# Layer 1, first pass: where the variance products and their transposes stand in the loop over strips

## The chip, the cores and the metric

The kernel runs on one core of a Trainium2 chip. The metric is the time of one execution on the device, in microseconds (us); lower is better. The engines are named as in the profile: PE is TensorE (PEld its weight loads), DVE is VectorE, ACT is ScalarE, POOL is GpSimd, and SP issues the DMAs.

## The reference

Two layers run one after the other on an image of 4 x 64 x 256 x 256 float32. Each adds to its input a function of the group-normed input. Layer 0 is a gated convolution with a small FFT; the change does not touch it. Layer 1 reads the image once along rows and once along columns as a sequence of 65,536 tokens of 64 channels, and does to each:

```python
fx = _layer_norm(x, ln1_g[i], ln1_b[i])            # over the 64 channels of a token
h = _s5_scan(fx, ...)                              # a linear recurrence forward and backward
x = jax.nn.gelu(h) + fx
fx2 = _layer_norm(x, ln2_g[i], ln2_b[i])
return fx2 @ ff_enc[i].T @ ff_dec[i].T + fx2
```

The two results are mixed by a 64 x 128 matrix and added to the input of the layer. What matters here is the first layer norm: the variance of each token over its 64 channels, one over its root, and the product with it.

## The kernel before, in words

For each of the four images, layer 1 runs `pass_a` (the layer norm, and a summary of each piece of 16 tokens for the recurrence), `scan` (the recurrence over the pieces) and `pass_b` (states, filter, second layer norm, output). The change is in `pass_a` alone.

`pass_a` goes over 16 strips of 16 rows. A strip lies in SBUF as 128 partitions (two halves of 64 channels) by 2048 elements, and is treated in four blocks of 512. Its steps:

- `centre(g, i)`: one matmul takes the mean off block i (`pc` in PSUM); ACT writes the centred values `xc` and their squares `sq`.
- `sums(g)`: four matmuls add the squares of the four blocks over the channels, all into one PSUM tile `pv`; ACT copies it to `sums`.
- `rstd_of(g)`: four PE transposes of `sums`, into another `pv` (the pool has one buffer of it); DVE adds the epsilon (`ve`); POOL raises to the power -0.5 (`rs`).
- `widen(g)`: DVE repeats these factors over 64 channels (`rw`, one buffer).
- `affine(g, i)`: four PE transposes bring the factors of block i to the layout of the data (`pr`, two buffers); DVE multiplies (`z`); ACT applies gain and bias twice, for columns (`fv`) and for rows (`fh`).
- `mirrored(s, g)`: SP stores `fv` and `fh`; DVE and POOL each make a sum and a difference of mirrored halves (`sd`, two operations on each engine).
- `summary_columns` and `summary_rows`, in two halves each: matmuls over `sd` into `pt` and `ps`, and with the second half an ACT copy `m` and DVE additions and subtractions `sf`, `sb`.

The steps run as a pipeline over strips. In iteration n, strip n is centred, strip n-1 gets its factors, strip n-2 its affine step, and strip n-3 its summaries; 16 + 3 iterations run for an image. Within an iteration, a loop over i = 0 to 3 interleaves one block of each (lines 1144 to 1156). [...] PE's instructions in this pass are pinned to the order of the program, and the other engines' queues show the same order, up to some small moves (the widening stands ahead of the `sd` of the same iteration, and the DVE work of the row summaries behind them).

The squares have five buffers, so a strip's four and one of the next fit.

Of the kernel before, what the change touches and what calls it, by code (L numbers as in the profile page):

```python
# [108 lines left out]
def tile_kernel(ctx: ExitStack, tc: tile.TileContext, x, cst, w0, winp, wdwp, w1, out):  # L109
# [74 lines left out]
    with ExitStack() as l0:  # L184
# [83 lines left out]
        with ExitStack() as l1w:  # L268
# [35 lines left out]
            def tmp(n=2, dt=F32):  # L304
                n_tmp[0] += 1
                return new(sp, [P, n], f"tmp{n_tmp[0]}", None, dt)
# [49 lines left out]
            def mul(a, b):  # L356
                o = tmp()
                TT(o, a, b, ALU.mult)
                return o
# [176 lines left out]
            u, t, r, i = mul(ur, ur), mul(ui, ui), tmp(), tmp()  # L536
# [9 lines left out]
            n = 1  # L546
# [456 lines left out]
    def load_strip(b, s):  # L1003
        t = new(ring, [P, 8, S], "strip")
        for h, r, row in rows_of(s):
            nc.sync.dma_start(out=t[h, r], in_=x1d[b][:, row : row + 7 : 2, :])
        return t
# [13 lines left out]
    def pass_a(b, x0):  # L1021
        with ExitStack() as es:
# [66 lines left out]
            def mirrored(s, g):  # L1089

                for d, n, e in ((1, 4, nc.vector), (0, 8, nc.gpsimd)):
                    f = g.pop("fv" if d else "fh")
                    nc.sync.dma_start(out=fxd[b][s, d], in_=f.rearrange("p a b -> p (a b)"))
                    for k, op in enumerate((ALU.add, ALU.subtract)):
                        t = g["sd", d, k] = new(wk, [P, n, 1024 // n], f"sd{d}", 3)
                        e.tensor_tensor(t, f[:, :n], f[:, : n - 1 : -1], op)  # L1096
# [43 lines left out]
            def at(s, step, *args):  # L1140
                if 0 <= s < NS1:
                    step(got[s], *args)

            for n in range(NS1 + 3):
                if n + 1 < NS1:
                    got[n + 1] = {"x": load_strip(b, n + 1)}
                for i in range(4):
                    at(n, centre, i)
                    if i == 1:
                        at(n - 1, rstd_of)  # L1150
                    at(n - 2, affine, i)
                    at(n - 3, (summary_columns, summary_rows)[i // 2], n - 3, i % 2)
                at(n, sums)
                if 0 <= n - 2 < NS1:
                    mirrored(n - 2, got[n - 2])
                at(n - 1, widen)
# [309 lines left out]
    for b in range(nb):  # L1466
        pass_a(b, first)
        first = pass_b(b)
# [77 lines left out]
```

## Time and profile before

| what | us |
|---|---|
| median of three runs | 9406.5 |
| lowest and highest of them | 9404.52 and 9409.52 |
| the profiled execution, its own time | 9404.9 |
| its span, from first to last instruction | 9403.1 |
| PE busy in the span | 8799.6 (94%) |
| DVE busy | 7346.4 (78%) |
| POOL busy | 3651.7 (39%) |
| ACT busy | 2785.1 (30%) |

The first matmul of `pass_a` starts at 4587.4, 5784.9, 6989.8 and 8193.7 us for the four images. All sums of an engine are over the whole span; `pass_a` has its own proportions, so its parts are read from stretches of the timeline. In the lines of the timeline the first number is the start in us from the beginning of the span, the second the time from the first start to the last end of the instructions merged in the line, and in square brackets stands the idle time of the engine just before, with what ended it. In the lines of waits, the numbers are the total in us, how often, and the longest. In lines by stretch, there are the length, then busy us and instructions of PE, PEld, DVE, ACT and POOL, the granted clock of PE as a share of its full one, the busy share of the DMA engines and GB/s.

### The profile page before, as it was taken

To read this page: it belongs to the slowest core of one execution; us is meant where nothing else is said; L and a number is where in the kernel's file an instruction comes from. 1 tells how busy PE (TensorE), PEld (TensorE's weight loads), DVE (VectorE), ACT (ScalarE), POOL (GpSimd) and SP (SyncE) were. 2 spreads that over 40 slices of the span, in tenths; PEclk is the share of its full clock that TensorE was granted. 3 is DMA by queue.
4 is the path that set the end of the run, shared out by engine and by line. 5 is a ranking of instruction groups with operands and counts; after the bars stand their busy time and mean duration, and the time that the engine had idled before them with its cause. 6 is when DMAs were issued, how large, how long until landed. Compare 5 with 4: busy or idle time off the path is not lost. (4 is left out here: it accounts for less than half of the span.)

```text
span 9403.1 us, 182768 instructions
## 1 busy us (share of the span) xinstructions
PE 8799.6 (94%) x78454; PEld 5836.8 (62%) x78454; DVE 7346.4 (78%) x8833; ACT 2785.1 (30%) x4570; POOL 3651.7 (39%) x2177
## 2 busy tenths in 40 slices
PE   3999999999999999999899999999999999999999
PEld 2666666666666666666556666556666566665666
DVE  7999989998999988888676776776767777677676
ACT  2222222222222222222452223522236222262222
POOL 4222222222222222222373444744446544375443
PEclk9999999999999999999999999999999999999999
DMA  7444444444434433333442234523346133362322
GB/s 170 97 95 99 99 94 97 97 96 96 99 95 99 97 85 84 83 81 77 121 159 67 78 90 115 183 55 86 79 104 202 50 85 86 86 195 72 90 77 72
DMA packets 655576, 938.40 MB, mean 100 GB/s; under 512 B 43184, under 2 KB 584880, under 8 KB 619184
## 3 DMA queue, kind: packets, MB, share of 16 engines
q1 hardware_dynamic: 654768, 926.71, 38.1%
q8 instruction: 619, 10.14, 0.5%
q14 instruction: 189, 1.55, 0.1%
HBM read 583.86 MB, written 275.05 MB: 91 GB/s over the span
## 5 line engine op out<-in xcount | busy, mean ns | idle before, releaser
L197 PE MATMUL m<-v,sw 64*128 64x256 f32 (+1 forms) x8192 | 1643.1, 414 | 209.6 <-DVE v L625 209.6
L197 PEld LDWEIGHTS m<-v,sw 64*128 64x128 f32 (+1 forms) x8192 | 1160.9, 200 | 769.7 <-DVE v L625 330.5
L1361 POOL TENSOR_TENSOR xr<-xr,fx 128x512 f32<-128x512 f32 x512 | 650.2, 1270 | 1861.7 <-ACT xr L1360 1371.1
L1258 PE MATMUL pst<-fx,wb 64*128 64x256 f32 (+1 forms) x4992 | 1015.9, 438 | 37.3 <-DVE stm L1264 18.3
L156 POOL TENSOR_SCALAR pn<-pr,nm,rs 128x512 f32<-128x512 f32 x256 | 387.5, 1521 | 1411.4 <-PE two L197 1406.2
L625 DVE SCALAR_TENSOR_TENSOR acc<-xat,taps,acc 128x1024 f32<-128x1024 f32 x640 | 831.0, 1298 | 4.6
L625 DVE SCALAR_TENSOR_TENSOR acc<-xen,taps,acc 128x1024 f32<-128x1024 f32 x384 | 750.1, 1953 | 4.5
L1258 PEld LDWEIGHTS pst<-fx,wb 64*128 64x128 f32 (+1 forms) x4992 | 508.1, 187 | 370.8 <-issue 244.2
L797 ACT ACTIVATE ge<-two 128x1024 f32<-128x1024 f32 x256 | 262.8, 1026 | 1593.8 <-PE two L197 1593.7
L1391 POOL TENSOR_TENSOR rs<-ve,mhalf 128x32 f32<-128x32 f32 x128 | 695.2, 5432 | 99.8 <-DVE ve L1264 99.8
L1264 DVE SCALAR_TENSOR_TENSOR stm<-stm,step,pst 128x512 f32<-128x512 f32 x640 | 478.4, 748 | 232.7 <-PE pst L1258 219.2
L197 PEld LDWEIGHTS m<-ct,hw 128*64 128x64 f32 x16384 | 510.6, 138 | 116.9 <-issue 116.9
L1362 ACT ACTIVATE sq<-xr 128x512 f32<-128x512 f32 x512 | 322.6, 630 | 874.5 <-POOL xr L1361 874.5
L1258 PE MATMUL px<-wb,xr 128*128 128x128 f32 x4096 | 574.8, 284 | 0.0
L1264 DVE SCALAR_TENSOR_TENSOR sto<-sto,step,pst 128x512 f32<-128x512 f32 x512 | 382.7, 747 | 242.7 <-PE pst L1258 228.8
L1258 PEld LDWEIGHTS px<-wb,xr 128*128 128x128 f32 x4096 | 524.8, 194 | 54.2 <-issue 41.8
L1264 DVE TENSOR_TENSOR y<-px,rs 128x512 f32<-128x512 f32 x512 | 353.7, 691 | 232.5 <-PE px L1258 222.7
L1258 PE MATMUL ph<-sto,wb 128*64 128x128 f32 (+1 forms) x5120 | 528.0, 299 | 0.0
L197 PE MATMUL m<-ct,hw 128*64 128x64 f32 x16384 | 527.8, 223 | 0.0
L1258 PE MATMUL ph<-stm,wb 128*64 128x128 f32 (+1 forms) x5120 | 525.0, 299 | 0.0
L1258 PEld LDWEIGHTS ph<-stm,wb 128*64 128x64 f32 (+1 forms) x5120 | 409.0, 147 | 144.6 <-issue 128.0
L1096 POOL TENSOR_TENSOR sd<-fh 128x1024 f32<-128x1024 f32 x128 | 380.3, 2991 | 298.4 <-PE pv L1034 225.4
(318 smaller groups left out, 16525.4 us busy)
## 6 DMA issues: line engine op xcount, KB each, us to landing
strip<-x1d SPq DMA_DIRECT2D x512, 256.0 KB, 7.3
fx<-fxd SPq DMA_DIRECT2D x128, 1024.0 KB, 7.0
at<-in_x_dram SPq DMA_DIRECT2D x248, 320.0 KB, 4.9
xen<-xat SPq DMA_DIRECT2D x256, 258.0 KB, 3.7
sx<-in_x_dram SPq DMA_DIRECT2D x256, 256.0 KB, 5.2
pr<-in_x_dram SPq DMA_DIRECT2D x256, 256.0 KB, 4.2
er<-in_x_dram SPq DMA_DIRECT2D x256, 256.0 KB, 4.7
x1d<-x SPq DMA_DIRECT2D x256, 256.0 KB, 3.6
```

Of the source, the lines that this page charges most:

```text
L156: nc.gpsimd.tensor_scalar(o, i, nm, rs, ALU.add, ALU.mult)
L197: tc.keep_in_program_order(nc.tensor.matmul(*args, **kw))
L625: return lambda *args, **kw: tc.keep_in_program_order(getattr(nc.vector, name)(*args, **kw))
L797: nc.scalar.activation(t["ge"], pg.rearrange("p e x -> p (e x)"), AF.Gelu)
L1096: e.tensor_tensor(t, f[:, :n], f[:, : n - 1 : -1], op)
L1258: tc.keep_in_program_order(nc.tensor.matmul(*args, **kw))
L1264: return lambda *args, **kw: tc.keep_in_program_order(getattr(nc.vector, name)(*args, **kw))
L1361: nc.gpsimd.tensor_tensor(xr, xr, fx, ALU.add)
L1362: nc.scalar.activation(sq, xr, AF.Square)
L1391: nc.gpsimd.tensor_tensor(r, ve.rearrange("p n c -> p (n c)"), mhalf, ALU.pow)
```

## The change

In the loop over blocks, `sums` leaves the end of the iteration: for strip n-1 it now runs in iteration n, in block 0 behind that block's `affine` of strip n-2. `rstd_of`, which stood in block 1 ahead of `affine`, now stands in block 1 behind it. The steps themselves are as they were.

```diff
                 for i in range(4):
                     at(n, centre, i)
-                    if i == 1:
-                        at(n - 1, rstd_of)
                     at(n - 2, affine, i)
+                    if i < 2:
+                        at(n - 1, (sums, rstd_of)[i])
                     at(n - 3, (summary_columns, summary_rows)[i // 2], n - 3, i % 2)
-                at(n, sums)
                 if 0 <= n - 2 < NS1:
                     mirrored(n - 2, got[n - 2])
                 at(n - 1, widen)
```

In the order of each engine's instructions, a steady iteration changes so. PE before: centre 0, affine 0, columns, centre 1, transposes of `sums`, affine 1, columns, centre 2, affine 2, rows, centre 3, affine 3, rows, products of the squares. PE after: centre 0, affine 0, products of the squares, columns, centre 1, affine 1, transposes of `sums`, columns, and the rest as before. ACT's copy of `sums` moves from ahead of block 0's `xc` to behind block 0's `fh`. On DVE `ve` moves from ahead of block 1's `z` to behind it. POOL's order does not change in steady iterations.

## The prediction

> **What bounds the kernel now.** I read the page first. TensorE is busy 94% of the span (8799.6 of 9403.1 us), but that is an average over stages, and the change touches one: pass_a, which runs four times, as the matmuls of `pc` (centre) show: from 4587.4, 5784.9, 6989.8 and 8193.7 us, some 280 us each. Then the groups by line: `pv<-sq`, the products of sums, wait 33.4 us in all for ACT's last square, and that is the wait the change takes apart. Whether it matters I asked of the waits and the timeline of one stretch where the passes run steadily, 4660 to 4820 (ten strips).
>
> ```profile
> L1034 PE MATMUL pv<-sq,ct 128*32 128x512 f32 x512 | 141.1, 605 | 34.2 <-ACT sq L1045 33.4
> ```
>
> ```profile
> ACT fv L1080 <- DVE ve L1061: 35.8, 10, 3.6
> DVE sf L1112 <- ACT m L1110: 34.4, 10, 3.4
> DVE sd L1096 <- ACT fv L1080: 14.9, 10, 1.5
> ...
> ACT fv L1080 <- DVE z L1076: 8.4, 10, 0.9
> ...
> PE pv L1034 <- ACT sq L1045: 5.6, 10, 0.6
> ```
>
> PE waits 0.56 us a strip. ACT and DVE wait for each other far longer, 3.6 + 0.9 and 3.4 + 1.5 us: the mark of a loop through both. The timeline of one strip shows it (start, duration):
>
> ```profile
> 4743.70 4.53 DVE L1096 TENSOR_TENSOR sd<-fv 128x1024 f32<-128x1024 f32 x2 [1.49 <-ACT fv L1080]
> ...
> 4744.53 0.59 ACT L1054 COPY sums<-pv 128x512 f32<-128x512 f32 x1
> ...
> 4747.98 0.60 PE L1038 MATMUL pv<-ct,sums 128*128 128x128 f32 x4
> ...
> 4748.95 1.02 DVE L1076 TENSOR_TENSOR z<-xc,pr 128x512 f32<-128x512 f32 x1
> ...
> 4750.00 0.81 ACT L1080 ACTIVATE fv<-z,prm 128x512 f32<-128x512 f32 x1 [3.58 <-DVE ve L1061]
> ...
> 4751.43 0.67 ACT L1044 ACTIVATE xc<-pc,norms 128x512 f32<-128x512 f32 x1
> ...
> 4753.98 0.35 ACT L1110 COPY m<-pt 128x256 f32<-128x256 f32 x1
> ...
> 4754.36 0.60 DVE L1112 TENSOR_TENSOR sf<-pt,m 128x256 f32<-128x256 f32 x1 [3.43 <-ACT m L1110]
> ...
> 4756.32 0.81 ACT L1080 ACTIVATE fv<-z,prm 128x512 f32<-128x512 f32 x1 [0.83 <-DVE z L1076]
> ...
> 4758.89 0.81 ACT L1080 ACTIVATE fv<-z,prm 128x512 f32<-128x512 f32 x1
> ...
> 4759.73 4.52 DVE L1096 TENSOR_TENSOR sd<-fv 128x1024 f32<-128x1024 f32 x2 [1.49 <-ACT fv L1080]
> ```
>
> From one `sd` to the next: sd and the four row results on DVE until z of block 0, 5.25; z to fv, 1.05; fv, fh, xc, sq, fv, fh on ACT until m, 3.98; m to sf, 0.38; sf, sb and z of block 2 until its fv, 1.96; fv, fh, xc, sq until fv of block 3, 2.57; fv to sd, 0.84. The sum is 16.03 us, the whole period. No PE instruction is in it. PE's 0.56 us is slack of an engine that the loop holds back. The reader should also see where the copy of `sums` stands: at 4744.53, in the 3.6 us in which ACT waits for z anyway. It costs nothing there.
>
> [...] fv waits 3.58 us and the xc behind it, whose input is long there, starts only after it. [...] at the end of the first pass a window with PE busy 1.25 of 3.41 us is followed by two at clock 0.50.
>
> ```profile
> 4834.83:4838.24 3.41, 1.25 (x16) 0.84 (x12) 2.71 (x3) 1.77 (x3) 2.39 (x2) 1.00 0.37 154
> 4838.24:4841.65 3.41, 1.03 (x3) 0.85 (x4) 3.41 (x2) 0.00 (x0) 3.41 (x2) 0.50 1.02 423
> ```
>
> I laid all windows of this grid against the clock that followed: those followed by a drop were at most 0.55 busy, those not followed by one at least 0.50. So about half busy is the bound. [...] two `sd` on DVE take 4.53 us when DVE starts first, and 6.65 us at 4837.20, where POOL's `sd` started 0.15 us earlier.
>
> **The change, part by part.** No instruction is added or removed. Per strip, sums (4 products, one ACT copy) goes from the end of the iteration to behind the first affine block of the next; rstd_of (4 transposes, `ve` on DVE, the power on POOL) goes behind the second affine block. The order of the two programs per engine bears this out. POOL's and SP's steady orders (load, two stores) stay.
>
> 1. *Removed:* the products' wait, 0.56 us plus about 0.2 of lost overlap (1.82 us unblocked against 2.6). It was slack: 0.
>
> 2. *The copy of sums.* ACT's order becomes fv, fh (block 0), sums, xc, sq. Behind a waiting fv, it can no longer use ACT's idle time. It ends, from sd: 5.25 + 1.05 + fv and fh 1.43 (4750.00 to 4751.43) + 0.63 (spacing 4744.53 to 4745.16) = 8.36 us. Queued behind it: xc, sq, fv, fh, m. By itself it lengthens the ACT-DVE loop by 0.63, to 16.66.
>
> 3. *The new wait.* PE's transposes wait for that copy, and behind them stands everything that the rest of the iteration needs. PE would be ready earlier: pc of block 0 starts 0.17 before sd (below), then pc 0.97, pr 0.43, sums 1.82, pt 1.73, pc 0.86, pr 0.60: ready at 6.24. The wait is 8.41 - 6.24, about 2.1 us. After it, by PE's starts in this trace: transposes 0.44, pt 1.73, pc 0.86, pr 0.53, ps 1.98, pc 0.96, pr of block 3 0.60 and 0.04 to DVE, 7.14 in sum. So z of block 3 starts at 8.36 + 7.14 = 15.50. Then z 0.90, widen (rw) 1.14 (4836.06 to 4837.20), and the next sd at 17.54. PE's ps behind that pr ends, and pc starts, at 15.50 - 0.64 + 0.53 + 1.98 = 17.37: the 0.17 used above. New period 17.54 against 16.03: +1.5. The loop now runs ACT, PE, DVE.
>
> 4. *Moved with it:* `ve` at about 9.2 stands ahead of sf, which waits for m until 11 anyway: nothing. The power on POOL starts at 9.36 (POOL's two sd are done near 6.8) and ends at 14.8, before z of block 3 is through at 16.4: nothing, with 1.6 us in hand. Without that cover widen and sd would slip by the difference. [...] DVE's sd starts 0.7 us before POOL's (fv, fh and 0.14 behind z against widen): stays at 4.5; if it flipped, +2.1.
>
> 5. *Clock.* A gap of 2.1 us leaves a window that holds 1.7 of it less than half busy, and the next, at half clock, falls on the chain of step 3: 3.41 / 2 = 1.7 us lost. Such a window catches the gap for 0.62 of all phases. 17.54 us is 5.14 windows, with a drop 5.64: the phase moves by 0.14 without and 0.64 with one, so one drop comes with (1 - 0.64) / 0.14 = 2.6 strips without: one in 3.6. Bounds: none, and one per strip.
>
> 6. *Sum of a pass.* Thirteen steady strips (4616.5 to 4824.2 is 13 now) x 1.5 = 19.5. Drops: 13 / 3.6 x 1.7 = 6.2. Start: sums of strip 0 now follow the first centre of strip 1, for whose load PE waits 4.3 to 4.9 us in the last three passes, so its transposes come some 2 us later, and the first affine to sd takes about 11.3 instead of 10.35 us (4605.85 to 4616.2): 3, an estimate from these rows. Drain: with no centre left, sd to sd becomes 8.41 + 0.64 + 0.17 + 0.14 + power 5.43 + 0.03 + widen 1.14 = 15.96 against 13.32 (4823.88 to 4837.20): 2.6. Together 31.3, four passes 125. On the profiled execution (9404.9 us, span 9403.1) that gives 9530; the median of the runs lies 1.6 above it: 9531.
>
> **Rivals.** A: as above, 9531, its own range 9495 to 9565. Chance 0.69.
> B: the transposes' wait is mostly absorbed and only the copy's 0.63 is paid: 4 x (13 x 0.63 + 5.6) = 55, 9462. For it: PE's durations of single matmuls are modelled, and 7.14 us may hide slack. Against: starts, not ends, were summed. 0.10.
> C: more: a drop in every strip, 13 x 1.7 = 22 per pass in place of 6.2, gives 9595[...]. Against: phases and the 0.7 us in hand. 0.11.
> D, on the other side: PE is what bounds the pass, the gap goes, and the period falls to the 15.26 us that the strip from 4616.48 to 4631.74, without a wait, takes: 12 x 0.77 x 4 = 37, 9369. PE's 97% (15.48 of 16.03 us) speaks for it; the closed loop of 16.03 without PE against it. It decides if the copy gets through before z of block 0, over 2.1 us earlier than worked out. 0.06.
> E: no change: copy and transposes land in slack, 9406. 0.04.
>
> **How the numbers follow.** The likeliest is A. To leave out no more than two in ten the range takes in B and the near part of C: 9460 to 9595. A difference of 0.2% (19 us) is about what can be told from none here: slower is A, B, C, 0.90; same 0.04; faster 0.06.
>
> **What would show it.** Right: a period near 17.5 us from sd to sd, with strips near 19.2 among them; PE idle some 2 us before the transposes, released by ACT's sums; no wait left before `pv<-sq`; ACT's sums right behind fh; clock 0.5 windows inside the pass. Wrong: a period of 16.0 or less, or 16.7 (B); 19 throughout, or sd pairs of 6.6 us (C). What would make it wrong altogether is fv of block 0 no longer waiting for z.

## The result and the profile after

| | before | after |
|---|---|---|
| median of four runs, us | 9405.51 | 9506.33 |
| lowest and highest | 9401.53 and 9409.52 | 9501.32 and 9507.91 |
| the profiled execution, its own time | 9404.9 | 9507.91 |
| its span | 9403.1 | 9506.1 |

The change makes the kernel slower, by a ratio of 1.0106 [1.0089, 1.0124]: 101 us, where 125 were forecast.

The page of the changed kernel, the span and the busy time of each engine:

```profile
span 9506.1 us, 182768 instructions
...
PE 8782.6 (92%) x78454; PEld 5840.1 (61%) x78454; DVE 7346.1 (77%) x8833; ACT 2808.8 (30%) x4570; POOL 3661.8 (39%) x2177
```

The number of PE's instructions is as before and its busy time is down by 17 us, yet the span is 103 us longer. The time did not go into work but into waiting. The groups by line say where (busy, mean ns of one; then idle time before, and what ended it):

```profile
L1034 PE MATMUL pv<-sq,ct 128*32 128x512 f32 x512 | 77.6, 681 | 0.0
...
L1038 PE MATMUL pv<-ct,sums 128*128 128x128 f32 x256 | 41.6, 286 | 128.7 <-ACT sums L1054 128.7
```

The 33 us for which the products waited on ACT's squares are gone, and the transposes behind them now wait 128.7 us for ACT's copy of `sums`. The waits in the stretch from 4660 to 4820 us, some nine strips, give the same; the longest wait is that of one strip (total, times, longest):

```profile
ACT fv L1080 <- DVE z L1076: 40.8, 27, 4.0
...
PE pv L1038 <- ACT sums L1054: 24.1, 9, 2.7
...
DVE z L1076 <- PE pr L1038: 22.3, 11, 2.4
```

Read in order these three lines point to a new loop: ACT waits for DVE's `z`, PE waits for ACT's copy, and DVE waits for PE's `pr`. `sd`, which before waited 1.5 us a strip for ACT, waits for nothing that is seen here. The timeline of one steady strip puts the loop in order (start, duration):

```profile
4703.69 4.53 DVE L1096 TENSOR_TENSOR sd<-fv 128x1024 f32<-128x1024 f32 x2
...
4705.05 1.06 PE L1034 MATMUL pv<-sq,ct 128*32 128x512 f32 x8
...
4708.94 1.88 DVE L1076 TENSOR_TENSOR z<-xc,pr 128x512 f32<-128x512 f32 x2
4709.98 0.81 ACT L1080 ACTIVATE fv<-z,prm 128x512 f32<-128x512 f32 x1 [3.99 <-DVE z L1076]
4710.70 0.80 ACT L1084 ACTIVATE fh<-z,prm 128x512 f32<-128x512 f32 x1
4711.40 0.56 ACT L1054 COPY sums<-pv 128x512 f32<-128x512 f32 x1
...
4712.02 0.66 PE L1038 MATMUL pv<-ct,sums 128*128 128x128 f32 x4 [2.68 <-ACT sums L1054]
...
4712.51 1.89 PE L1034 MATMUL pt<-sd,wa 128*128 128x256 f32 x8
...
4714.24 1.02 PE L1034 MATMUL pc<-strip,cenr 128*128 128x512 f32 x2
...
4718.57 0.60 PE L1038 MATMUL pr<-ct,rw 128*128 128x128 f32 x4
...
4719.21 1.04 DVE L1076 TENSOR_TENSOR z<-xc,pr 128x512 f32<-128x512 f32 x1 [2.37 <-PE pr L1038]
...
4720.10 1.21 DVE L1068 COPY rw<-rs 128x2048 f32<-128x2048 f32 x1
...
4721.22 4.52 DVE L1096 TENSOR_TENSOR sd<-fv 128x1024 f32<-128x1024 f32 x2
```

The products are done at 4706.1, but ACT copies them only at 4711.40, behind `fv` and `fh` of block 0. For nearly four of these five us ACT stands idle in front of `fv`. PE starts its transposes at 4712.02, 8.33 us after `sd`, and from there it has no wait up to `pr` of block 3, so that its own work sets the pace: 7.19 us to `z` of block 3, then 0.89 to `rw` and 1.12 to the next `sd`. The period is 17.53 us; it was 16.03.

Every third strip is longer. PE's clock shows why; first two windows of the stretch before the strip above (length; busy us and instructions of PE, PEld, DVE, ACT, POOL; granted clock; DMA share; GB/s), then the timeline in them:

```profile
4690.39:4693.80 3.41, 1.00 (x7) 0.95 (x8) 1.40 (x3) 3.04 (x5) 0.87 (x2) 1.00 0.86 219
4693.80:4697.21 3.41, 3.41 (x9) 2.36 (x8) 0.30 (x1) 1.89 (x4) 3.41 (x1) 0.50 0.00 0
```

```profile
4684.47 4.53 DVE L1096 TENSOR_TENSOR sd<-fv 128x1024 f32<-128x1024 f32 x2
...
4692.80 0.66 PE L1038 MATMUL pv<-ct,sums 128*128 128x128 f32 x4 [2.68 <-ACT sums L1054]
...
4693.29 3.12 PE L1034 MATMUL pt<-sd,wa 128*128 128x256 f32 x8
...
4696.20 1.53 PE L1034 MATMUL pc<-strip,cenr 128*128 128x512 f32 x2
```

The wait falls into one window, which is then 1.00 of 3.41 us busy, and the next runs at clock 0.50: `pt` takes 3.12 us instead of 1.89, `pc` 1.53 instead of 1.02. From this `sd` to that at 4703.69 it is 19.22 us. Four of the twelve steady strips of each pass are so. In those of the first pass half clock is granted from 4639.19, 4693.80, 4748.41 and 4820.09 us on, each time for 3.41 us, and these starts lie 16, 16 and 21 times 3.41 us apart.

The whole difference by parts, in us, each the sum of the four passes. The first `sd` ends the start; the thirteen strips run from the first to the fourteenth `sd`; the drain ends where the scan begins:

| part of the difference | forecast | measured |
|---|---|---|
| start, to the first `sd` | +12 | +25.7 |
| thirteen strips, clock included | +102.8 | +95.6 |
| drain | +10.4 | -6.9 |
| outside these | 0 | -11.4 |
| sum, in the span | +125 | +103 |

### The profile page after: what moved, and what is told of

It reads as the page before. It is cut to its first block, busy times and chain, and to the rows that moved or that the text cites. A ratio compares the mean times of both kernels' runs of the same rounds, so it can differ in the third digit from the quotient of the medians.

```text
span 9506.1 us, 182768 instructions
## 1 busy us (share of the span) xinstructions
PE 8782.6 (92%) x78454; PEld 5840.1 (61%) x78454; DVE 7346.1 (77%) x8833; ACT 2808.8 (30%) x4570; POOL 3661.8 (39%) x2177
## 5 line engine op out<-in xcount | busy, mean ns | idle before, releaser
L1257 PEld LDWEIGHTS ph<-sto,wb 128*64 128x64 f32 (+1 forms) x5120 | 404.9, 147 | 143.0 <-issue 129.7
```

What stands on the lines that cost most here:

```text
L1257: tc.keep_in_program_order(nc.tensor.matmul(*args, **kw))
```

## The experiments

Each was timed beside the kernel before on the same chip; ratios are to that.

**1. The copy off ACT's queue.** The theory: PE's wait is only for the place of the copy behind a waiting `fv`. Give the copy to another engine, and leave the products and transposes where the change puts them.

```diff
-                nc.scalar.copy(g["sums"], ps)
+                nc.vector.tensor_copy(g["sums"], ps)
```

> The kernel after, with its copy of sums made by DVE in place of ACT; PE's order is unchanged. Theory (the loss is the copy's place behind fv and fh in ACT's queue): DVE makes it right behind z of block 0, some 6.2 us after sd starts, PE's transposes start near 6.8 instead of 8.3, PE's wait falls from 2.7 to about 1.5 us, PE's leg no longer ends last, the period from sd to sd returns to about 16.0 us and no half-clock windows are left in the steady part: 9405 to 9425 us. Rival (the places of the products and transposes in PE's order are what costs): the period stays near 17.5, 9490 us or more.

Measured: 9435.4 against 9402.22, ratio 1.0037 [1.0022, 1.0052]. The timeline of a strip of it:

```profile
4702.86 1.00 DVE L1076 TENSOR_TENSOR z<-xc,pr 128x512 f32<-128x512 f32 x1
...
4703.72 0.67 DVE L1054 COPY sums<-pv 128x512 f32<-128x512 f32 x1
...
4704.44 0.66 PE L1038 MATMUL pv<-ct,sums 128*128 128x128 f32 x4 [1.17 <-DVE sums L1054]
```

The copy follows `z` directly, PE still waits, but 1.17 us and not 2.68, and the period is back at 16.02 to 16.08 with no half-clock window among the steady strips. The steady part is what the theory says. The total is above the expected one: in this kernel the first `sd` comes 5.3 to 9.3 us later than in the kernel before. So the start is a cost of its own, whichever engine copies.

**2. The copy on ACT, ahead.** Experiment 1 also adds work to DVE. This one changes ACT's order alone: `affine` is cut in two behind `z`, so that the copy can be given to ACT before `fv` and `fh`, and these are pinned in that order. The orders on PE, DVE and POOL are those of the changed kernel.

```diff
-                nc.scalar.copy(g["sums"], ps)
+                tc.keep_in_program_order(nc.scalar.copy(g["sums"], ps))
...
-                    if i < 2:
-                        at(n - 1, (sums, rstd_of)[i])
+                    if i == 0:
+                        at(n - 1, sums)
+                    at(n - 2, gains, i)
+                    if i == 1:
+                        at(n - 1, rstd_of)
```

Here `gains` holds the two ACT operations (`fv`, `fh`) that stood at the end of `affine`.

> The kernel after with one thing altered: ACT's copy of sums stands ahead of fv and fh of block 0 in ACT's queue. The orders of PE, DVE and POOL are those of after, instruction for instruction. Theory (the copy behind the waiting fv is the whole of the steady loss): period 16.0 us, PE's wait before the transposes gone, no half-clock windows in the steady part; what is left is the start of a pass, 3 to 8 us each as in the two kernels run first: 13 to 32 us over before. Rival (the new places on PE, or ve behind z of block 1 on DVE, take part): period clearly over 16.1 us, over 40 us slower than before.

Measured: 9414.98 against 9404.17, ratio 1.0013 [1.0006, 1.002]. A strip of it, from `sd` to `sd`:

```profile
4700.24 4.52 DVE L1100 TENSOR_TENSOR sd<-fv 128x1024 f32<-128x1024 f32 x2 [1.50 <-ACT fv L1084]
...
4702.22 0.59 ACT L1054 COPY sums<-pv 128x512 f32<-128x512 f32 x1
...
4704.65 0.60 PE L1038 MATMUL pv<-ct,sums 128*128 128x128 f32 x4
...
4706.54 0.82 ACT L1084 ACTIVATE fv<-z,prm 128x512 f32<-128x512 f32 x1 [3.73 <-DVE z L1076]
...
4716.29 4.52 DVE L1100 TENSOR_TENSOR sd<-fv 128x1024 f32<-128x1024 f32 x2 [1.49 <-ACT fv L1084]
```

The copy runs in the 3.73 us for which ACT waits anyway, PE does not wait for it, no window among the steady strips is at half clock, and the old loop with its old period of 16.01 to 16.07 is back. Moving one 0.59 us copy ahead of two instructions of its own engine takes back some 90 of the 101 us. This settles where the loss of the steady strips comes from. What is left, 11 us, is the start (the first `sd` comes 4.4 to 6.6 us later in each pass) less a shorter first strip and a shorter drain.

**3. Both steps ahead of `affine`.** The products and the transposes stand in the same blocks as after the change, but each in front of that block's `affine`.

```diff
-                    at(n - 2, affine, i)
                     if i < 2:
                         at(n - 1, (sums, rstd_of)[i])
+                    at(n - 2, affine, i)
```

> The kernel after with the two steps ahead of affine in blocks 0 and 1 instead of behind it: the products still stand behind the next strip's first centre, so PE's wait for the last square is gone as in after, but ACT's copy stands ahead of fv again. Theory (the loop through DVE and ACT sets the period, PE's wait was slack): period 16.0 us, 9400 to 9415 us, no gain over before although the wait is gone. Rival (PE bounds the pass): period near 15.3, 9368 us. Rival (the products' new place costs by itself): 9450 us or more.

Measured: 9418.41 against 9402.22, ratio 1.0017 [1.001, 1.0024], a little above what was expected. PE no longer waits for the squares in the steady strips, and the period is 16.02 to 16.06 all the same. The wait that the change removes was slack: without it and without the new wait nothing is gained. Most of the 16 us by which this kernel is slower lies at the start again: its first `sd` comes 1.3 to 5.1 us later in each pass, 13 us in all.

**4. Work in the gap.** The theory of the clock: the longer strips come only of the window that the gap leaves with little to do. The transposes of block 1 are given six times over, to the same result, so that PE works through its wait.

```diff
-                turn_blocks(ps, lambda k: g["r"][:, 8 * k + 2 * i : 8 * k + 2 * i + 2].rearrange("p a c -> p (a c)"))
+                for _ in range(6 if i == 1 else 1):
+                    turn_blocks(ps, lambda k: g["r"][:, 8 * k + 2 * i : 8 * k + 2 * i + 2].rearrange("p a c -> p (a c)"))
```

> The kernel after, with the four transposes of affine block 1 issued six times over instead of once (same result each time): 5 x 0.44 = 2.2 us more PE work ahead of the transposes of sums, all of it inside PE's wait of 2.7 us. Theory (the 19.2 us strips are half-clock windows that the gap brings): the period is 17.5 us in every strip, the four long strips per pass are gone, and the run is 4 x 4 x 1.7 = 27 us faster than after: about 9479 us. Rival (drops come from something else): 19.2 us strips remain, 9506 us. Rival (more PE work pushes the transposes back): slower than 9506 us.

Measured: 9502.95 (9500.1 to 9512.83) against 9402.22, ratio 1.0109 [1.0094, 1.0124]. A strip of it:

```profile
4710.99 2.78 PE L1038 MATMUL pr<-ct,rw 128*128 128x128 f32 x24
...
4713.68 0.56 ACT L1054 COPY sums<-pv 128x512 f32<-128x512 f32 x1
...
4714.29 0.66 PE L1038 MATMUL pv<-ct,sums 128*128 128x128 f32 x4 [0.52 <-ACT sums L1054]
```

PE works 2.78 us where it stood still, waits 0.52, and no window among the steady strips is at half clock: each of them takes 17.54 to 17.62 us, none 19.2. The thirteen strips take 226.5 to 227.8 us a pass instead of 231.4 to 231.9. So the drops are made by the gap. But the expected gain in the total was not there: the first strip of each pass takes 15.7 to 17.1 us instead of 14.3 to 14.8, the pass lengths sum to only 12 us less, and the medians of this kernel and of the changed one are not told apart. That the drops cost some 27 us (16 of 1.69) is seen in the steady strips, not in a total.

**5. The first strips as before.** In iterations 0 to 2 the two steps keep their old places; from the third on the change holds.

```diff
+                    if i == 1 and n <= 2:
+                        at(n - 1, rstd_of)
                     at(n - 2, affine, i)
-                    if i < 2:
+                    if i < 2 and n > 2:
                         at(n - 1, (sums, rstd_of)[i])
...
+                if n < 2:
+                    at(n, sums)
```

> The kernel after, with sums and rstd_of of strips 0 and 1 in their old places; from strip 2 on as in after. Theory (the start costs more than the 3 us that the prediction gave it, because sums of strip 0 waits with PE behind the load of strip 1 and drops of the clock follow): the first sd comes some 4 to 8 us earlier in a pass than in after, the steady period is still 17.5 with some 19.2; about 75 to 88 us slower than before in place of 101. Rival (the late first sd has another cause): as slow as after.

Measured: 9483.78 against 9404.17, ratio 1.0087 [1.0072, 1.0102]: 80 us over the kernel before, where the changed kernel is 101 us over. The first `sd` is at 29.3, 35.4, 35.0 and 37.0 us after the start of its pass, close to where it was before the change (28.8, 35.8, 35.6, 35.0), and the steady strips are still 17.53 with some of 19.2. What the change costs at the start shows when the second pass is laid beside the same pass of the changed kernel. First the changed kernel, PE's timeline:

```profile
5818.27 2.05 PE L1034 MATMUL pc<-strip,cenr 128*128 128x512 f32 x2 [9.14 <-DMA strip<-x1d]
...
5823.80 0.60 PE L1038 MATMUL pv<-ct,sums 128*128 128x128 f32 x4
...
5831.58 1.12 PE L1038 MATMUL pr<-ct,rw 128*128 128x128 f32 x4 [3.83 <-DVE rw L1068]
...
5837.21 0.63 PE L1038 MATMUL pv<-ct,sums 128*128 128x128 f32 x4
```

Then the one with the first strips as before:

```profile
5813.32 3.36 PE L1034 MATMUL pc<-strip,cenr 128*128 128x512 f32 x4 [6.43 <-DMA strip<-x1d]
5816.52 0.60 PE L1038 MATMUL pv<-ct,sums 128*128 128x128 f32 x4
...
5824.30 0.66 PE L1038 MATMUL pr<-ct,rw 128*128 128x128 f32 x4 [1.67 <-DVE rw L1068]
...
5825.65 0.60 PE L1038 MATMUL pv<-ct,sums 128*128 128x128 f32 x4
```

From the arrival of strip 1 the first transposes start after 5.53 us against 3.20. But the second, those of strip 1, start 5.63 us after the first `pr` against 1.35. At the start POOL's power, 5.4 us, stands bare between transposes and `rw`, so both delays go into the first `sd`: 2.3 and 4.3 of the 7.9 us by which it is later here. In the second of them PE is at half clock in the changed kernel alone: the same `pr` takes 1.12 us there and 0.66 here.

**6. The loop itself.** The prediction took the closed loop through DVE and ACT to be the bound before the change. If it is, then shortening it, in the kernel before, should bring the gain that removing PE's wait could not. DVE's second `sd` is put behind block 0's `z` of the next iteration, so that `fv` no longer has both in front of it; the row additions follow the first `sd` in a step of their own, and the DVE operations concerned are pinned.

```diff
                     at(n - 2, affine, i)
+                    if i == 0:
+                        at(n - 3, second)
...
                     mirrored(n - 2, got[n - 2])
+                at(n - 3, add_rows, n - 3)
                 at(n - 1, widen)
```

> The kernel before, with DVE's second sd moved behind z of the next strip's block 0, and the row results pinned between the first sd and that z; nothing else moves. Theory (DVE's 4.5 us of sd[...] stand in the loop through DVE and ACT): z of block 0 starts about 2 us after sd instead of 5.25, the loop is no longer the last to end, and PE's own work bounds a strip at 14.6 to 15.3 us: 13 x 0.7 to 1.4 x 4 = 40 to 75 us faster than before, 9330 to 9368 us. Rival (PE's wait for the square is the bound in before): the period stays at 16.0, 9405 us. Rival (the later sd keeps z of block 1 or the column products waiting): 9405 us or slower.

Measured: 9329.3 (9322.48 to 9332.18) against 9402.22, ratio 0.9923 [0.9907, 0.994]: 73 us faster than the kernel before, faster than both. The timeline of a strip, and below it a stretch of ten strips by engine:

```profile
4701.16 1.21 DVE L1101 TENSOR_TENSOR sd<-fv 128x1024 f32<-128x1024 f32 x1
...
4703.61 1.04 DVE L1076 TENSOR_TENSOR z<-xc,pr 128x512 f32<-128x512 f32 x1 [0.45 <-PE pr L1038]
...
4704.50 1.21 DVE L1101 TENSOR_TENSOR sd<-fv 128x1024 f32<-128x1024 f32 x1
4704.69 0.81 ACT L1080 ACTIVATE fv<-z,prm 128x512 f32<-128x512 f32 x1 [0.24 <-DVE z L1076]
...
4715.59 1.22 DVE L1101 TENSOR_TENSOR sd<-fv 128x1024 f32<-128x1024 f32 x1
```

```profile
4660.00:4804.40 144.40, 144.40 (x1165) 105.47 (x1164) 93.10 (x141) 119.86 (x190) 114.69 (x31) 1.00 0.69 219
```

`fv` waits 0.24 us where it waited 3.6, the period is 14.43 us, and PE, whose busy time has modelled ends, is busy for all of the 144.40 us (139.34 in the kernel before). Its timeline has no wait in this stretch: now PE is the bound of the pass. Here its wait for squares is gone too, as a result and not as the means. The two `sd`, which took 4.53 us as a pair, take 1.21 each.

A second run of the same kernel. Its label speaks of the change, but the kernel is that of the split alone:

> The kernel with the second sd behind z, run again for a second look at its trace: period 14.4 us, about 73 us faster than before.

Measured: 9327.0 against 9404.17, again with a period of 14.43. One run only: it repeats the result and decides nothing new.

**7. The change on top of the split.** Now PE bounds the pass, so a wait of PE, or an order of its work that takes longer, would count. The two steps of the change are put into the split kernel by the same diff as in the case itself.

> The change made on top of the kernel with DVE's second sd behind z of block 0. Theory (the change costs what the copy's place behind fv costs, and that depends on how late z of block 0 is): z of block 0 starts some 2.4 us after sd in place of 5.25, so the copy ends near 5.4, when PE is about ready for the transposes; the period is 14.4 to 14.9 us, and only the start of a pass is paid: 10 to 50 us slower than the split kernel, 40 us or more faster than before. Rival (the change costs 1.5 us or more a strip wherever z stands): period 16 or more, 9405 us or slower.

Measured: 9362.91 against 9404.17, ratio 0.9957 [0.9942, 0.9972]: 41 us faster than the kernel before, where the split alone is 73 us faster. The period is 14.63 instead of 14.43 and PE has no wait in front of the transposes: `fv` of block 0 starts at 4705.26, the copy behind it runs from 4706.68 for 0.57 us, and PE comes to the transposes at 4707.75. Over the thirteen strips that is 3.1 us a pass, 12 in all. The 0.2 us a strip lie in PE's own order, by the timelines of the two: the products start 0.53 us after a `pr`, where `pt` starts 0.43 after it, and `pc` starts 1.83 us after a `pt` that stands behind the products, 1.73 after another. Why these steps differ is not shown. The larger part is the start: the first `sd` comes 3.7 to 7.8 us later in each pass, 26 us in all. The split kernel has no wait for the squares left that the change could take away, so only its costs are seen here.

## Why the prediction was right

**Step 1, the wait that goes, at nothing:** right. Experiments 2 and 3 have neither the old wait nor the new one, and are not faster than the kernel before. Its size was put too low, at 0.56 us and 0.2 of lost overlap. In the kernel before, the eight records of the products stand in two groups:

```profile
4741.39 1.06 PE L1034 MATMUL pv<-sq,ct 128*32 128x512 f32 x6
...
4743.02 1.05 PE L1034 MATMUL pv<-sq,ct 128*32 128x512 f32 x2 [0.57 <-ACT sq L1045]
```

That is 2.68 us from the first start to the last end, against 1.06 after the change: 1.6 us of slack a strip, of which only 0.57 is seen as a wait. It is also the difference between the period of 16.03 and the 14.43 us that PE needs in experiment 6. So PE's 97% busy in these strips was no sign that PE is the bound.

**Step 2, the copy behind `fv` and `fh`:** right. It was to end 8.36 us after `sd`; its end, 0.56 us after 4711.40, is 8.27 after. Experiment 2 shows that its place is the whole cause of the steady loss.

**Step 3, the new wait and the period:** right where it counts, 17.54 forecast and 17.53 measured. PE's leg was taken as 7.14 us and is 7.19. The wait itself was put at 2.1 us and is 2.68, because the products were taken at 1.82 us and take 1.06. That moves the start of the wait, not its end, so the period did not notice.

**Step 4, `ve`, the power and the two `sd`:** right. POOL's power runs from 4712.98 for 5.43 us and is through before `z` of block 3 at 4719.21; DVE's pair stays at 4.5 us (4.53 at 4703.69).

**Step 5, the clock:** the cause is shown by experiment 4, and the sum was near: 3.6 drops of 1.7 us a pass forecast, 4 of 1.69 measured. In part this is luck, for two terms were off and offset each other. The gap was put at 2.1 us and is 2.68. The bound was put at half busy; in the steady strips of the changed kernel, the 16 windows at full clock that a drop followed had PE 0.20 to 0.39 busy, so none of them was idle, and the other 216 at least 0.42. An estimate from these figures: with a bound of 0.4 a window has to hold 2.05 us of the gap, and it does so in (3.41 + 2.68 - 2 x 2.05) / 3.41 = 0.58 of all phases, where the step had 0.62; a gap of 2.68 us with a bound of half would have given 0.79. The busy share alone does not decide it everywhere: behind each pass, in `scan`, one window with PE 0.62 to 0.69 busy was followed by a drop.

**Step 6, the sum of a pass:** the two ends were mis-sized, in opposite directions, 14 us too little and 17 too much over the four passes. That they nearly cancel is luck, so the nearness of 101 to 125 us says less for the prediction than its steady strips do. Of the thirteen strips, the first does not have the new period: it takes 14.3 to 14.8 us, against 15.2 before. That takes some 9 us off the forecast of 102.8, and the drops bring 2 more than forecast.
- *Start*, forecast 3 a pass, measured 6.4. The step charged the delay of strip 0's factors alone. Strip 1's stand behind the new places too, and experiment 5 shows the two delays one after the other.
- *Drain*, forecast +2.6 a pass, measured -1.7. The step laid the steady queue of ACT over iterations that have no centring any more. There the copy stands ahead of `fv` again, as ACT's timeline of the changed kernel shows:

```profile
4849.27 0.59 ACT L1054 COPY sums<-pv 128x512 f32<-128x512 f32 x1 [1.13 <-PE pv L1034]
4853.59 0.81 ACT L1080 ACTIVATE fv<-z,prm 128x512 f32<-128x512 f32 x1 [3.74 <-DVE z L1076]
```

  So the first strip of the drain takes 13.87 us and not 15.96. In the next, DVE's pair starts 0.68 us ahead of POOL's and takes 4.51 us, where in the kernel before POOL's started 0.15 us ahead and DVE's took 6.65; that strip is 12.3 instead of 14.5 to 15.0 us. The flip that was weighed as a risk happened, the other way round and in another place.
- *Outside* the thirteen strips and the two ends lie another 11 us in favour of the changed kernel. 4.7 of them are ahead of the first pass and the others between the passes and behind them, where the two programs are the same; they are not put down to the change, and their cause is open.

The rivals: B (only the 0.63 us of the copy) fell to the period and to PE's wait; C (a drop in every strip, or DVE's longer pair of `sd`) to strips of 17.53 and pairs of 4.5; D and E to the result. D had named the right engine at the wrong time: PE does bound this pass at 14.4 us, but only once the loop through DVE and ACT is opened.

## What to carry to other kernels

Before an engine's wait is removed, add up the loop that sets the period; if the starts sum to it without that engine, its wait is slack, however large its busy share, and the gain lies in the loop (here in one `sd` moved behind the `z` that ACT waits for). When a step is moved in a program, look at every queue it is moved in: a copy of 0.6 us that stood in an idle gap cost 1.5 us a strip when it came to stand behind an instruction that waits, because another engine waited for it. Work the start and the end of a pipeline out on their own queues, since the steady order does not hold there.

## What the runs showed of the hardware

- Four products of 32 output columns, eight records, take 1.06 us together when all operands are ready; the one product of `pc`, with the same 512 columns, takes 1.02. The records overlap in the trace: after the change 512 of them, of 681 ns on average, lie in 77.6 us of busy time. With the last operand 0.57 us late, before the change, the four took 2.68 us, and the two late records alone took 1.05, as long as all eight together: most of what the late operand costs is overlap that is lost, and not the wait that the profile shows.
- A gap of 2.68 us in 17.5 us of otherwise dense work on PE was enough for half a clock in one window of some sixteen (three strips), each 1.69 us; filled to 0.52 us it cost none.
- Two DVE operations of 1.21 us each (experiment 6) take 4.53 us as a pair when POOL starts its own between their starts. In the strip at 4743.70 of the kernel before, the first takes 1.23 us, and the second, which starts at 4744.84 while POOL's first runs (from 4744.51 for 2.64 us), takes 3.38. Here it costs over 2 us a strip for a matter of order, and with the pair pulled apart, in experiment 6, it is gone from DVE: both take 1.21 us, the second at 4704.50 with POOL's pair running from 4701.88 for 6.07 us.
